# A two-layer graph transformer on one core: gather distance and raw chunks of layer 2, and the order of work at the ends of the span

## The chip, the cores and the metric

One core of a Trainium2 chip runs the whole program. A core has five engines that work side by side, each through its own instruction stream in order: TensorE (PE in the profile; PEld are its weight loads), VectorE (DVE), ScalarE (ACT), GpSimd (POOL) and SyncE (SP). DMAs are issued from SP, ACT and POOL, and 16 DMA engines carry them out. The metric is the device time of one execution in microseconds (us), as a median of runs.

## What is computed

The reference takes 6250 nodes with 128 features, and 106,250 edges sorted by their destination `dst`, each with 64 attributes and a weight. An edge's attributes are joined with 32 cosines of a time difference; two attention layers with two heads follow, with a normalisation over all nodes and a relu between them; at the end the input is added and each node's row is normalised.

```python
def _transformer_conv(h, edge_attr, src, dst, Wq, bq, Wk, bk, Wv, bv, We, Ws, bs):
    q, k, v = ((h @ W + b).reshape(n, H, C) for W, b in ((Wq, bq), (Wk, bk), (Wv, bv)))
    e = (edge_attr @ We).reshape(-1, H, C)
    alpha = einsum('ehc,ehc->eh', q[dst], k[src] + e) / sqrt(C)
    ex = exp(alpha - segment_max(alpha, dst)[dst])
    a = ex / segment_sum(ex, dst)[dst]
    return segment_sum((v[src] + e) * a[:, :, None], dst).reshape(n, H * C) + h @ Ws + bs

rel_t = last_update[src] - t
edge_attr = concatenate([cos(rel_t[:, None] * time_w + time_b), msg], axis=-1)
h = _transformer_conv(x, edge_attr, src, dst, ...)
h = relu((h - h.mean(0)) / sqrt(((h - h.mean(0)) ** 2).mean(0) + 1e-05) * bn_g + bn_b)
out = layernorm(x + _transformer_conv(h, edge_attr, src, dst, ...))
```

## The kernel before

The planning stage in `tile_gnn_resnorm` cuts the sorted edges into 106 chunks (`NC`) of at most 1024 edges (8 rows of 128, `T`) and 64 destination nodes. It tests that the input fits this plan; here it does, and `ordered` runs (`general` is the way for other inputs and isn't run).

**The planning stage** also makes what layer 1 starts from. `load_features` (L505) loads x in four pieces of 12 blocks each into the tile `fhT` from SP's queue, with the times of the nodes behind the first piece, and last the rows left over (`fxrest`, L515 to L517). `pass_features` (L520) writes x with the times in front to the DRAM table `xv_d`: the left-over rows first (L528), then the four pieces, each copied by VectorE or ACT in turn (L530) and stored from SP (L531). It is a generator, and the lines from L1306 on decide where its steps fall between the first table (`tables`, L622, also a generator, with five steps), the edge indices (`columns`, L1312) and the rest.

**Layers 1 and 2** are two calls of `conv` (c = 0 and 1), each a loop of rounds (L964) in which the order of every engine is written by hand. In round k:

- `fetch` (L720) loads the edge attributes of a chunk to come into its buffer `ff`, and its table `ftab`; in layer 2 also the encoded times, the turned edge attributes of layer 1 (`et_d`) and the residual rows (L738 to L744).
- `gather` (L746) fetches the source nodes' rows with eight indirect DMAs from POOL, one for 128 edges. `bring` (L971) places them over the round and ties most to a step of TensorE (`behind`), so that they keep its pace. `lead` (L758) says how many chunks ahead: 4 in layer 1, 2 in layer 2. The buffer `ff` exists five times in layer 2.
- `score(k, 0)`, `turn_weights(k - 1)` and `score(k, 1)` are matmuls for the chunk's scores and the transposes of the weights of the chunk before; `lowest` and `weigh` (VectorE, ACT) make the exponentials; `turn_in(k + 1, ·)` transposes the gathered rows of the next chunk; `divide`, `finish_turn` and `finish` close chunk k - 2; `gather_sums(k - 1)` (L867) sums chunk k - 1 by sixteen matmul instructions.
- `pull(extra, n)` (L1019) takes n steps of other work: in layer 1 the tables of later nodes and, near the end, `pass_rows` or `put_rows`, which transpose finished columns of `fhT` and store them as rows of `h_d`; in layer 2 `block` (L1145): a table block in four steps, then the residual rows, then steps with nothing, seven in all.

Layer 2's nodes are read from two tables. `h_d` holds the raw results of layer 1. `hn_d` holds them after normalisation and relu. It is made in 13 row blocks by `hide` (L769: four transposes on TensorE, a copy on VectorE into one of four `fhn` buffers, a store from SP), three blocks in the round before round 0 and five each in rounds 0 and 1 (L1017). The first `RAW` = 4 chunks are gathered from `h_d` instead, and get the normalisation afterwards, in `turn_in` for the scores and by three VectorE operations in `normalise` (L883) for the sums.

**The end.** `finish` of layer 2 subtracts each row's mean; the squares' sum is closed for a group of chunks at once by a Sqrt on ACT (L939 to L941). `STARTS` lists the first chunk of each group: ten chunks a group up to 96, then 97 to 101, 102 to 104, and 105. `store` (L945) scales a closed chunk on ACT and stores it from SP, one to four a round (L1028). Neighbouring chunks overlap in `out`, so each store waits for the one before.

Of the kernel before, what the change touches and what calls it, by code (L numbers as in the profile page):

```python
# [13 lines left out]
P = 128  # L14
# [30 lines left out]
T = 8  # L45
CE = T * P
NN = P // H
NC = 106
# [7 lines left out]
HIGHEST = 2.0 ** 119  # L56

LG = 10
STARTS = (*range(0, 91, LG), 97, 102, 105)


@with_exitstack
# [439 lines left out]
def load_features(nc, pl, mw, x, node_vec):  # L502

    N = x.shape[0]
    NF = N // P  # L505
    NR = N - NF * P
    xall = pl.xall = pl.hT[:, :NF * D].rearrange("p (b d) -> p b d", d=D)
    pl.cuts = list(zip(range(0, NF, 12), [*range(12, NF, 12), NF]))
    for b0, b1 in pl.cuts:
        nc.sync.dma_start(xall[:, b0:b1], x[:NF * P, :].rearrange("(p b) d -> p b d", b=NF)[:, b0:b1])  # L510
        if b0 == 0:
            pl.times = mw.tile([P, NF], F32, name="fnv", bufs=1)
            nc.sync.dma_start(pl.times, node_vec[:NF * P].rearrange("(p b) -> p b", b=NF))
    if NR:
        nc.vector.memset(pl.rest, 0.0)  # L515
        nc.sync.dma_start(pl.rest[:NR, 1:], x[NF * P:N, :])
        nc.sync.dma_start(pl.rest[:NR, 0:1], node_vec[NF * P:N].rearrange("(p a) -> p a", a=1))  # L517


def pass_features(nc, pl, mw, dram, N):  # L520

    NF = pl.xall.shape[1]
    pl.xv_d = dram.tile([N, 1 + D], F32, name="xv_d")
    rows = mw.tile([P, NF, 1 + D], F32, name="fxrows", bufs=1)
    nc.vector.tensor_copy(rows[:, :, 0], pl.times)
    to = pl.xv_d[:NF * P, :].rearrange("(p b) d -> p b d", b=NF)
    if N > NF * P:
        nc.sync.dma_start(pl.xv_d[NF * P:N, :], pl.rest[:N - NF * P])  # L528
    for i, (b0, b1) in enumerate(pl.cuts):
        (nc.scalar.copy if i % 2 else nc.vector.tensor_copy)(rows[:, b0:b1, 1:], pl.xall[:, b0:b1])  # L530
        nc.sync.dma_start(to[:, b0:b1], rows[:, b0:b1])  # L531
        yield

# [127 lines left out]
def ordered(ctx: ExitStack, tc: tile.TileContext, pl, x, dst, edge_attr_64, conv2, bn_g, bn_b, out):  # L661
# [30 lines left out]

    SINGLE = 40

    RAW = 4

    hidden = list(range(-(-N // GE)))

    def conv(c, extra, first_blocks=None):
# [56 lines left out]
        shape = [P, T, TD]  # L756

        def lead(k):  # L758
            return 2 if c else AHEAD

        def yield_first(bring):
            if not c:
                bring(range(T))
                return
            bring(range(5))
            bring(range(5, T), pl.step)
            first_blocks()
# [66 lines left out]
        def score(k, u):  # L834

            s = ch[k]
            if u == 0:
                s.ps = p_s.tile([P, CE], F32, name="fps")
            w = slice(u * GE, (u + 1) * GE)
            half = nc.tensor.matmul(s.ps[:, w], s.tab[:, :, 0], s.ft[:, w], start=True, stop=False)  # L840
            return half, nc.tensor.matmul(s.ps[:, w], s.tab[:EC, :, 1], s.et[:, w], start=False, stop=True)  # L841
# [120 lines left out]
        with cs, tc.manual_schedule():  # L962
            ended = None
            for k in range(-lead(-NC), NC + 3):  # L964
                def on(j):
                    return 0 <= j < NC

                coming = [j for j in range(k + lead(k - 1), k + lead(k) + 1) if on(j)]
                filling = False

                def bring(rows, behind=None):  # L971
                    for j in coming:
                        gather(j, rows, behind)

                for j in coming:
                    fetch(j)
                if k == -lead(-NC):
                    yield_first(bring)
                elif k < -1:
                    bring(range(T))  # L980
                elif not filling:
                    bring(range(1), ended)
                step = score(k, 0)[1] if on(k) else hide(1) if c and k == -1 else None
                if k >= -1 and not filling:
                    bring((1,), step)
                step = turn_weights(k - 1) if on(k - 1) else hide(1) if c and k == -1 else None
                if k >= -1 and not filling:
                    bring((2,), step)
                place()
                if on(k - 2):  # L990
                    divide(k - 2)
                half, step = score(k, 1) if on(k) else (hide(1) if c and k == -1 else None, None)
                if k >= -1 and not filling:
                    bring((3,), half if c else step or half)
                    if c:
                        bring((4,), step)
                if on(k - 2):
                    finish_turn(k - 2)
                if on(k):
                    lowest(k)  # L1000
                step = turn_in(k + 1, 0) if on(k + 1) else None
                if k >= -1 and not c:
                    bring(range(5) if filling else (4,), step)
                if on(k):
                    weigh(k)
                step = turn_in(k + 1, 1) if on(k + 1) else None
                if k >= -1:
                    bring((5,), step)
                for j in (k + 2,) if k < SINGLE else (k + 2, k + 3) if k == SINGLE else (k + 3,):
                    if c == 0 and on(j):  # L1010
                        encode(j)
                        if j < SINGLE + 3:
                            sine()
                if k >= 0:
                    at_round[0] = k
                    if c and k < 2:
                        hide(5)  # L1017
                    else:
                        pull(extra, 2 if k < 4 or k > 96 else 1)  # L1019
                if len(args) == 3 or args and k == NC - 4:  # L1020
                    sine()
                if on(k - 2):
                    finish(k - 2)
                if c and on(k):
                    if k < RAW:
                        normalise(k)
                    nc.vector.tensor_copy(ch[k].f[:, :, 1 + D:1 + D + TD], ch[k].z)
                for _ in range(min(len(done), 4 if k >= NC else 2 if k > NC - 12 else 1)):  # L1028
                    store(*done.pop(0))
                *steps, ended = gather_sums(k - 1) if on(k - 1) else (None, None, None)  # L1030
                if k >= -1:
                    for t, step in zip((6, 7), steps):
                        bring((t,), step)
            at_round[0] = 2 * NC
            for _ in extra:
                pass
            for rows in done:
                store(*rows)
# [146 lines left out]
def tile_gnn_resnorm(ctx: ExitStack, tc: tile.TileContext, x, src, dst, edge_attr_64, edge_weight, node_vec,  # L1185
# [13 lines left out]
    with tc.tile_pool(name="plan", bufs=1) as pl, tc.tile_pool(name="planw", bufs=2) as mw, \  # L1199
# [140 lines left out]
        next(first_table)  # L1340
        next(first_table)
        next(passed)
        for _ in first_table:
            pass
        columns(flats[0], srcs)
        for _ in passed:
            pass
        got.tw = broadcast(nc, keep, "ftw", time_w, TD)
        got.tb = broadcast(nc, keep, "ftb", time_b, TD)
        nc.sync.dma_start(got.wv[0], conv1["Wv"])  # L1350
# [55 lines left out]
```

## Time and profile before

Three runs: median 2306.39 us, from 2305.79 to 2308.45. The execution that was profiled took 2306.31 us.

| what | us |
|---|---|
| the profiled execution, device time | 2306.31 |
| its span, first to last instruction | 2304.3 |
| granted TensorE clock, mean over the span | 0.983 |
| planning, layer 1's first gather on POOL | 39.25 |
| layer 1's last gather from xv_d | 1132.2 |
| layer 2's first gather from h_d | 1184.96 |
| layer 2's first gather from hn_d | 1232.29 |
| layer 2's last gather | 2266.08 |
| last store issued | 2298.65 |

| stretch, us | TensorE busy | VectorE busy | ACT busy | POOL busy | granted clock | DMA share |
|---|---|---|---|---|---|---|
| 0 to 60 | 34.61 | 30.89 | 19.25 | 20.87 | 0.77 | 0.74 |
| 300 to 700 | 397.62 | 281.33 | 272.33 | 295.91 | 1.00 | 0.64 |
| 1100 to 1180 | 74.53 | 43.46 | 39.55 | 25.20 | 1.00 | 0.39 |
| 1180 to 1240 | 45.12 | 29.50 | 26.40 | 36.60 | 0.86 | 0.82 |
| 1240 to 1300 | 56.29 | 25.08 | 20.09 | 42.66 | 0.97 | 0.71 |
| 1700 to 2000 | 296.10 | 117.81 | 133.25 | 226.90 | 1.00 | 0.68 |
| 2240 to 2270 | 25.74 | 7.78 | 10.56 | 18.68 | 0.89 | 0.59 |
| 2270 to 2304 | 20.26 | 10.68 | 12.06 | 0.00 | 0.87 | 0.04 |

A line of a group in the profile reads: line of the code, engine, operation, tile written and tile read, count, then busy time, mean length of one in ns, and the idle time of that engine just before, with what ended most of it. A line of a timeline reads: start, length, engine, line, operation, tiles, count, and in brackets the idle time before it. Busy time isn't the whole cost of an instruction: the step from one to the next on the engine counts too.

### The profile page before, as it was taken

The numbers are of one execution on the slowest core, as the hardware profiler recorded it, in microseconds if no ns is written. First come the engines' busy times: TensorE is split into PE (matmuls) and PEld (weight loads), VectorE is DVE, ScalarE is ACT, GpSimd is POOL, SyncE is SP. The second block draws the span as 40 slices with busy tenths as digits, with TensorE's granted clock in tenths as the row PEclk, the third lists the DMA queues.
The fourth block names the chain that finished last, engine by engine and source line by source line (L and its number), as shares of the span: only waits on it lengthen the run. The fifth ranks groups of instructions, "written<-read, shape, count | busy, mean of one in ns | idle before, by whom it ended". The sixth has DMA issues, their size and how long they took to land.

```text
span 2304.3 us, 40495 instructions
## 1 busy us (share of the span) xinstructions
PE 2210.9 (96%) x11589; PEld 1707.9 (74%) x11589; DVE 1243.7 (54%) x3745; ACT 1227.9 (53%) x1951; POOL 1628.7 (71%) x1717
## 2 busy tenths in 40 slices
PE   5999999999999999999978999999999999999996
PEld 3687888778887888888856777777777776777775
DVE  5576767676676767777635333433334343343332
ACT  3677777776666665555643444444444444444443
POOL 3777777777777777777536777777777777777772
PEclk7899999999999999999989999999999999999998
DMA  7666666656666666666548656676676676666562
GB/s 231 167 179 171 173 190 178 187 143 180 187 176 179 160 191 172 179 179 168 146 121 219 172 153 181 184 183 174 170 190 184 173 188 165 178 180 162 152 168 51
DMA packets 431095, 396.64 MB, mean 172 GB/s; under 512 B 279682, under 2 KB 375167, under 8 KB 427535
## 3 DMA queue, kind: packets, MB, share of 16 engines
q1 hardware_dynamic: 357648, 239.69, 38.1%
q0 software_dynamic: 54656, 113.07, 20.5%
q10 hardware_dynamic: 18558, 41.20, 5.0%
q8 instruction: 95, 1.56, 0.3%
q14 instruction: 138, 1.12, 0.2%
HBM read 277.16 MB, written 113.14 MB: 169 GB/s over the span
## 4 chain that ended last, share of the span: by engine, by line
PE 67%; DMA 6%; POOL 2%; issue 2%; DVE 1%; SPq 0%; ACT 0%; POOLq 0%; DVEq 0%; ACTq 0%
PE fpa L871 22%; PE fps L840 11%; PE fps L841 11%; PE fpx L819 6%; PE fppt L863 6%; DMA ff<-hn_d,fsrcs 5%; PE fpg L627 3%; PE fpe L828 2%; POOL ff L749 2%; PE fpo L921 2%; PE fpo L922 1%; PE fpo L893 1%; PE fpo L894 1%; PE fpo L903 1%; PE fpo L904 1%
## 5 line engine op out<-in xcount | busy, mean ns | idle before, releaser
L749 POOL DMA_INDIRECT ff<-xv_d,fsrcs x848 | 817.7, 964 | 304.0 <-issue 100.0
L749 POOL DMA_INDIRECT ff<-hn_d,fsrcs x816 | 775.6, 950 | 265.4 <-issue 107.1
L871 PE MATMUL fpa<-ff,fpt 128*128 128x225 f32 x3392 | 693.3, 357 | 0.0
L871 PEld LDWEIGHTS fpa<-ff,fpt 128*128 128x128 f32 x3392 | 627.4, 190 | 11.2 <-issue 0.7
L864 ACT COPY fpt<-fppt 128x512 f32<-128x512 f32 x424 | 228.0, 590 | 472.2 <-PE fppt L863 467.4
L840 PE MATMUL fps<-fft,ftab 128*128 128x512 f32 x848 | 442.9, 604 | 0.6 <-ACT fs L853 0.6
L823 ACT COPY fft<-fpx 128x512 f32<-128x512 f32 x416 | 242.1, 582 | 365.3 <-PE fpx L819 365.2
L896 DVE COPY fat<-fpo 128x256 f32<-128x256 f32 x212 | 90.1, 425 | 586.0 <-PE fpo L894 556.3
L853 ACT ACTIVATE fs<-fps,fm 128x1024 f32<-128x1024 f32 x212 | 236.3, 1114 | 85.8 <-DVE fm L848 83.4
L819 PE MATMUL fpx<-fident,ff 128*128 128x128 f32 x1696 | 248.2, 276 | 34.6 <-DMA ff<-hn_d,fsrcs 26.3
L863 PEld LDWEIGHTS fppt<-fident,fs 128*128 128x128 f32 x1696 | 198.4, 141 | 104.7 <-issue 103.6
L846 DVE TENSOR_REDUCE flow<-fps 128x1 f32<-128x1024 f32 x212 | 257.5, 1214 | 10.0 <-PE fps L841 10.0
L819 PEld LDWEIGHTS fpx<-fident,ff 128*128 128x128 f32 x1696 | 197.9, 141 | 46.4 <-DMA ff<-hn_d,fsrcs 34.3
L841 PE MATMUL fps<-fxT,ftab 112*128 112x512 f32 x424 | 218.4, 596 | 2.1 <-DMA fxT<-et_d 2.1
L863 PE MATMUL fppt<-fident,fs 128*128 128x128 f32 x1696 | 220.0, 272 | 0.0
L841 PE MATMUL fps<-fet,ftab 112*128 112x512 f32 x424 | 217.9, 595 | 0.0
L840 PEld LDWEIGHTS fps<-fft,ftab 128*128 128x128 f32 x848 | 166.6, 226 | 3.8 <-issue 2.2
L841 PEld LDWEIGHTS fps<-fet,ftab 112*128 112x128 f32 x424 | 106.5, 251 | 76.0 <-issue 58.7
L841 PEld LDWEIGHTS fps<-fxT,ftab 112*128 112x128 f32 x424 | 83.9, 198 | 102.0 <-issue 94.9
L794 DVE SCALAR_TENSOR_TENSOR farg<-fturns,farg 128x256 f32<-128x256 f32 x318 | 135.4, 426 | 10.9
L878 DVE TENSOR_SCALAR finv<-fpa 128x1 f32<-128x1 f32 x212 | 33.5, 158 | 191.7 <-PE fpa L871 185.3
L828 PE MATMUL fpe<-fident,ff 128*112 128x128 f32 x848 | 129.1, 275 | 1.5 <-DVE ff L806 1.5
(216 smaller groups left out, 2348.6 us busy)
## 6 DMA issues: line engine op xcount, KB each, us to landing
ff<-in_edge_attr SPq DMA_DIRECT2D x212, 256.0 KB
et_d<-fet SPq DMA_DIRECT2D x106, 448.0 KB
fxT<-et_d SPq DMA_DIRECT2D x106, 448.0 KB
ftab<-tab_d SPq DMA_DIRECT2D x106, 192.0 KB
tab_d<-fo ACTq DMA_DIRECT2D x13, 1536.0 KB
ff<-xv_d,fsrcs POOLq DMA_INDIRECT x848
enc_d<-fzs SPq DMA_DIRECT2D x106, 128.0 KB
ftab<-tab_d SPq DMA_DIRECT2D x106, 128.0 KB
```

The costliest lines, as they stand in the source:

```text
L749: row = nc.gpsimd.indirect_dma_start(out=f[:, t, (1 if c else 0):1 + D], out_offset=None, in_=(h_d[:N, :] if k < RAW else hn_d) if c else ...
L794: nc.vector.scalar_tensor_tensor(arg, turn, -part, arg, op0=OP.mult, op1=OP.add)
L819: last = nc.tensor.transpose(px[:, t * P:(t + 1) * P], s.f[:, u * 4 + t, 1:1 + D], ident)
L823: nc.scalar.copy(s.ft[:, u * GE:(u + 1) * GE], px)
L828: last = nc.tensor.transpose(pe[:EC, t * P:(t + 1) * P], s.f[:, u * 4 + t, 1 + D:], ident)
L840: half = nc.tensor.matmul(s.ps[:, w], s.tab[:, :, 0], s.ft[:, w], start=True, stop=False)
L841: return half, nc.tensor.matmul(s.ps[:, w], s.tab[:EC, :, 1], s.et[:, w], start=False, stop=True)
L846: nc.vector.tensor_reduce(low, s.ps, AX.X, OP.min)
L853: nc.scalar.activation(s.s, s.ps, AF.Exp, bias=s.bias, scale=-1.0)
L863: last = nc.tensor.transpose(pp[:, t * P:(t + 1) * P], s.s[:, at:at + P], ident)
L864: nc.scalar.copy(s.pt[:, u * GE:(u + 1) * GE], pp)
L871: nc.tensor.matmul(s.pa, s.pt[:, t * P:(t + 1) * P], s.f[:, t, 1:1 + D + EW], start=t == 0, stop=t == T - 1)
```

## The change

- **Distance and raw chunks.** `lead` is 3 in layer 2, and `RAW` is 6, so the first six chunks are gathered from `h_d`. The fill before round 0 takes three steps: chunk 0 as before; chunk 1, its eight gathers in pairs between three row blocks; chunk 2 behind the transposes of chunk 0 (`filling`).
- **Row blocks.** Three before round 0, then four, three and three in rounds 0, 1 and 2. The table steps that stood in rounds 2 and on begin in round 3: three there, two each in rounds 4 and 5, then one as before.
- **End of layer 1.** In its round `NC + 1` the two steps of `extra` (the row blocks 11 and 12 of `h_d`) also stand ahead of `finish_turn` and `finish` of the last chunk.
- **Start.** The left-over rows and their times are loaded ahead of x. The fourth piece of `xv_d` is copied by VectorE and not by ACT, after the first table's third step and ahead of its last steps and of the edge sources.
- **End.** The last groups are 97 to 100, 101 and 102, and 103, 104 and 105 alone.

```diff
 LG = 10
-STARTS = (*range(0, 91, LG), 97, 102, 105)
+STARTS = (*range(0, 91, LG), 97, 101, 103, 104, 105)
...
     pl.cuts = list(zip(range(0, NF, 12), [*range(12, NF, 12), NF]))
+    if NR:
+        nc.vector.memset(pl.rest, 0.0)
+        nc.sync.dma_start(pl.rest[:NR, 1:], x[NF * P:N, :])
+        nc.sync.dma_start(pl.rest[:NR, 0:1], node_vec[NF * P:N].rearrange("(p a) -> p a", a=1))
     for b0, b1 in pl.cuts:
...
-    if NR:
-        nc.vector.memset(pl.rest, 0.0)
-        nc.sync.dma_start(pl.rest[:NR, 1:], x[NF * P:N, :])
-        nc.sync.dma_start(pl.rest[:NR, 0:1], node_vec[NF * P:N].rearrange("(p a) -> p a", a=1))
...
-        (nc.scalar.copy if i % 2 else nc.vector.tensor_copy)(rows[:, b0:b1, 1:], pl.xall[:, b0:b1])
+        (nc.scalar.copy if i == 1 else nc.vector.tensor_copy)(rows[:, b0:b1, 1:], pl.xall[:, b0:b1])
...
-    RAW = 4
+    RAW = 6
...
         def lead(k):
-            return 2 if c else AHEAD
+            return 3 if c else AHEAD
...
-                filling = False
+                filling = c and k == -1
...
                     yield_first(bring)
+                elif k < -1 and c:
+                    for t in range(0, T, 2):
+                        bring((t, t + 1), hide(1) if t else None)
                 elif k < -1:
...
-                step = score(k, 0)[1] if on(k) else hide(1) if c and k == -1 else None
+                step = score(k, 0)[1] if on(k) else None
...
-                step = turn_weights(k - 1) if on(k - 1) else hide(1) if c and k == -1 else None
+                step = turn_weights(k - 1) if on(k - 1) else None
...
-                half, step = score(k, 1) if on(k) else (hide(1) if c and k == -1 else None, None)
+                if c == 0 and k == NC + 1:
+                    at_round[0] = k
+                    pull(extra, 2)
+                half, step = score(k, 1) if on(k) else (None, None)
...
-                if k >= -1 and not c:
+                if k >= -1 and not c or filling:
                     bring(range(5) if filling else (4,), step)
...
-                    if c and k < 2:
-                        hide(5)
+                    if c and hidden:
+                        hide(4 if k == 0 else 3)
                     else:
-                        pull(extra, 2 if k < 4 or k > 96 else 1)
+                        pull(extra, (3 if k == 3 else 2) if c and k < 6 else 2 if k < 4 or k > 96 else 1)
...
         next(passed)
+        next(first_table)
+        for _ in passed:
+            pass
         for _ in first_table:
             pass
         columns(flats[0], srcs)
-        for _ in passed:
-            pass
```

## Prediction

> **What bounds the kernel now.** I read the engine shares and slices first, then the groups by line, the stretches by engine, the gather engine's own timeline, the chain of waits, and last the queues at both ends of the span.
>
> ```profile
> PE 2210.9 (96%) x11589; PEld 1707.9 (74%) x11589; DVE 1243.7 (54%) x3745; ACT 1227.9 (53%) x1951; POOL 1628.7 (71%) x1717
> L749 POOL DMA_INDIRECT ff<-hn_d,fsrcs x816 | 775.6, 950 | 265.4 <-issue 107.1
> L819 PE MATMUL fpx<-fident,ff 128*128 128x128 f32 x1696 | 248.2, 276 | 34.6 <-DMA ff<-hn_d,fsrcs 26.3
> ```
>
> TensorE at 96% looks like the bound. In layer 1 it is: from 300 to 1050 us it idles 2.4 us. In layer 2 the second line decides. A row gather keeps POOL 0.95 us and 0.30 us lies before the next one even when nothing is waited for, so 1.25 us a gather, 10.0 us for a chunk's eight; POOL's 71% counts only the 0.95. A round of TensorE lasts 9.28 us without a piece of tables (sums at 1262.45, 1271.73, 1281.01 in the chain of waits) and 10.14 us with one (1311.99 to 1322.13). Of the seven pulls per table block five carry TensorE work, so a round means (5 x 10.14 + 2 x 9.28)/7 = 9.89 us, under POOL's 10.0. So layer 2 is bound by gather issue, and TensorE's waits (third line) are its shadow. What can be won there is POOL's real idle time:
>
> ```profile
> 1223.82 0.95 POOL L749 DMA_INDIRECT ff<-h_d,fsrcs  x1 [0.30 <-PE fpa L871]
> 1225.07 0.95 POOL L749 DMA_INDIRECT ff<-h_d,fsrcs  x1 [0.30 <-issue]
> 1232.29 0.95 POOL L749 DMA_INDIRECT ff<-hn_d,fsrcs  x1 [6.27 <-DMA hn_d<-fhn]
> 1233.54 0.95 POOL L749 DMA_INDIRECT ff<-hn_d,fsrcs  x1 [0.30 <-PE fpx L819]
> ...
> 2251.37 0.94 POOL L749 DMA_INDIRECT ff<-hn_d,fsrcs  x1 [0.67 <-PE fpx L819]
> 2254.22 0.95 POOL L749 DMA_INDIRECT ff<-hn_d,fsrcs  x1 [1.90 <-PE fpa L871]
> 2255.69 0.95 POOL L749 DMA_INDIRECT ff<-hn_d,fsrcs  x1 [0.53 <-PE fpa L871]
> ```
>
> The bracket is idle time and what ended it; 0.30 is the normal gap. Over the 848 gathers from 1184.96 to 2266.08 the excess above 0.30 sums to 17.9 us: 1.2 at 1192.41 (chunk 0), 6.0 for the normalised rows (above), 3.2 at 1253.51, 1.1 at 1336.60, 0.7 at 1470.06, 1.2 at 1605.43, 2.6 from 2251 to 2259, and 1.9 in eleven small ones. Both ends:
>
> ```profile
> SPq L528 <- DMA fxrest<-in_node_vec: 14.1, 1, 14.1
> 38.72 1.02 ACT L653 COPY fxT<-fpx 128x512 f32<-128x512 f32 x1 [10.13 <-DMA xv_d<-fxrows]
> ...
> 2290.19 2.36 SPq L956 DMA_DIRECT2D out<-fout  x2
> 2295.59 0.47 SPq L956 DMA_DIRECT2D out<-fout  x1
> 2298.65 0.48 SPq L956 DMA_DIRECT2D out<-flast  x1
> ```
>
> At the start SP stands 14.1 us for a tiny load that lies last in its queue, then the copies wait for the xv_d writes behind it. At the end the last store leaves at 2298.65, though its rows were ready at 2295.31: it waits for the store before it.
>
> **The change, part by part.** Everything is taken off the profiled execution: 2306.31 us, its span 2304.3 plus 2.0 around it, which equals the median 2306.39 within 0.1.
>
> *Three chunks ahead, six raw chunks, rows in three rounds.* Gathers and their pacing steps keep their number; chunk k+3 is issued where k+2 was. In the fill the order of POOL is the old one (chunks 0, 1, 2, 3 back to back from 1184.96 to 1225.07), so the 1.2 us of chunk 0 stay. Chunks 4 and 5 now read raw rows: the 6.0 us go. Chunk 6 is the first to need hn_d; POOL reaches it at 1226.3 + 2 x 10.0 = 1246.3. The last hn_d store now stands on SP behind the fetch of chunk 5 in round 2, whose buffer frees at the end of the sums of chunk 0 (about 1225); register reads, five issues and four stores (4.4 us a fetch in the rows at 1232 to 1237, 0.4 to 0.9 a store) bring it to about 1231, landed by about 1235, since the last one in the trace was issued at 1228.2 and released POOL at 1232.29. So 11 us of cover.
>
> The other 10.7 us are gathers that waited for TensorE. They can wait no more if POOL runs late against its pace. Starts of TensorE's rounds, worked forward from 1199.0 (round 0): the rounds 0 to 2 hold four, three and three row blocks (about 0.76 us each), round 3 three table pieces, round 4 two; I get 1213, 1225, 1236, 1248, 1259, 1268. POOL starts the chunk of rounds 1 to 6 at 1226, 1236, 1246, 1256, 1266, 1276: 7 to 13 us late each time, and gains another 7 x 10.0 - 69.3 = 0.7 us of lateness per table block. TensorE first waits when that lateness passes about 11 us (a row is allowed 8.2 us into round k-2 and needed 5 us into round k: 18.6 + 5 - 8.2 less some 4 of landing); before it was about 2. So POOL never stops, and TensorE waits for it once the slack is used. TensorE alone would be done sooner (101 rounds x 9.28 + 12 x 4.37 of tables = 990 us from 1236, against POOL's 1013), so it isn't the bound. Layer 2: -(6.0 + 10.7) = -16.7 us. Bounds: -10 if half of the small waits come back, -20 if the few gathers of 1.1 to 1.5 us also fall.
>
> The last row of chunk 105 then starts at 2266.08 - 16.7 = 2249.4. Before, its transposes ended 5.0 us after it (2271.1), not waiting for it. Now they do: a row landed 2.5 us after its start at 2233.51, at worst 7.07 (2243.51, two fetches at once). I take 3.5, nearer to the first since fetches are now held a round apart by their buffer, plus 0.5 to transpose: -1.0 (from -2.0 to +2.6). The Trainium skill, "DMA: Bandwidth & Descriptors", Anatomy of one DMA, gives 2.0 us plus bytes over 436e3, which is an estimated 2.15 us for 64 KB; with it the total would be 1.4 us lower.
>
> Hidden edits, at nothing: three VectorE operations more for chunks 4 and 5 (2 x 1.22 + 0.69 = 3.1 us each), under VectorE's 35 idle us between 1240 and 1300; without that cover 3.1 us a round. Row blocks, table pieces: only moved. The fetch now waits on SP for the sums of k-2, behind it the tab, z, et and residual loads and the round's output store: needed three rounds later, 20 us of cover. VectorE's memset waits for the same sums as the division behind it does anyway.
>
> *Start.* Loads keep DMA full to 22 us, then it falls to 0.39 and 0.26 until SP's wait ends at 24.28, and the writes run from 26 to 38. With the small loads first, the first three writes can start by 22 and the fourth is copied by VectorE near 24.8 and not by ACT at 27.12 to 28.59. The writes and the table (3.1 + 1.6 MB at some 420 GB/s, as from 26 to 36 us) then end near 33. The two small loads now push the x loads back by their issue, 0.27 + 0.44 us; the first copy, at 9.71, follows VectorE's own work and covers it. But VectorE's planning ends at 33.95 and takes the 0.95 us copy on top, so the xT copies start about 35.1 instead of 38.72: -3.6 (from -5 to +1, the copy's cost if nothing lands earlier). Layer 1 is bound by TensorE fed from these, so it passes through.
>
> *End of layer 1.* Two row blocks leave 1.0 us earlier on SP, ahead of the last hT store (1179.79) and of the h_d rows (1181.43), on which the first gather waits. VectorE's two copies (0.89) push the last result by 0.3: -0.8. Bound: TensorE now stands at these transposes until the hT store of 1173.09 landed, at the latest 1176.81 where they ran unhindered: +0.95; the other end -1.2.
>
> *Tail.* Chunk 104 closes alone, so its store leaves near 2289.8 and not 2295.59, and the last one goes when ready. Price: the close of chunk 103 puts a table load (1.28) and Sqrt between VectorE's statistics and the division of chunk 104: reciprocal at 2284.45, division at 2284.75 and not 2284.14, +0.7 on the closing chain. Last store 2295.31 + 0.7 + 0.4 = 2296.4 against 2298.65: -2.2 (from -3 to +1). A rule speaks against it: the Trainium skill, "ScalarE: Activation LUTs", What ACT_TABLE_LOAD costs, asks to group by table set and prices a switch at 2.66 us with its drain. The trace shows 1.283 us and Exp 0.02 us after its load (2272.73 to 2272.75), no drain; two switches more would by the rule be up to 5.3 us and the tail +3.
>
> Sum: -16.7 - 1.0 - 3.6 - 0.8 - 2.2 = -24.3; 2306.3 - 24.3 = **2282 us**.
>
> **Rivals.** *The waits come back* (the change does less than it says): gathers still stop at TensorE's pace because the five buffers are exactly full; only the 6.0 and the 3.2 go, the ends give 6.6: 2306.3 - 15.8 = 2290. For it: a gather of k+3 needs the buffer of k-2, free only as the round begins. Against: POOL is 7 us late there. *TensorE becomes the bound*: were the 0.30 gap a wait that lead removes, layer 2 ends 22 us earlier still, 2260. Against: 0.30 is the least gap in layer 1 too. *Nothing gained*: if what POOL wins is lost to slower landings, 2305. *SP sets the round*, the slower side: its fetch can no longer run ahead of the sums; if a fetch (4.4) and store (2 at most) took over 10.24 us a round, 102 rounds x 0.24 eat the 24 us; at 10.5 it is 2306.3 - 24.3 + 51 = 2333. The rows add to 6.4 us, so far from it.
>
> **Chances.** Forecast 0.78, own range 2276 to 2290; waits come back 0.13; TensorE bound 0.03; nothing 0.02; SP 0.04. A measurement here tells 0.2% (4.6 us) from no change. Faster 0.94, same 0.02, slower 0.04. Range 2274 to 2295: the forecast with its unknown landings and ends, and the first rival.
>
> **What would show it.** Right: 48 gathers from h_d and 800 from hn_d; no wait for hn_d before the first of these; POOL's gaps at 0.30 from chunk 1 to chunk 105; its last gather about 21 us earlier (layer 2 and both earlier ends); TensorE still waiting on gathered rows; xT copies near 35; the last two stores over 6 us apart. Wrong: gaps on POOL ended by TensorE in rounds 3 to 100, TensorE waiting for fxT, ftab or fr, a wait for hn_d at chunk 6, or a last store held by ACT's tables.

## The result and the profile after

The changed kernel takes 2288.26 us, median of six runs (2284.05 to 2289.69); the kernel before took 2306.56 (2303.14 to 2310.41) in the six runs beside it. The ratio is 0.9916, 95% interval 0.9905 to 0.9928: 18 us faster, 6 less than the 24.3 of the forecast. The six runs stand at two places, two near 2284.2 and four from 2288.1 to 2289.7; the profiled one is of the lower (2284.39, its span 2282.6).

The page of the changed kernel, engine shares and two groups by line:

```profile
PE 2204.2 (97%) x11589; PEld 1705.5 (75%) x11589; DVE 1244.6 (55%) x3756; ACT 1230.0 (54%) x1954; POOL 1625.4 (71%) x1717
...
L749 POOL DMA_INDIRECT ff<-hn_d,fsrcs x800 | 758.7, 948 | 243.8 <-issue 85.9
...
L819 PE MATMUL fpx<-fident,ff 128*128 128x128 f32 x1696 | 245.3, 275 | 26.1 <-DMA ff<-hn_d,fsrcs 15.7
```

The idle time before an hn_d gather was 265.4 us over 816 gathers and is 243.8 over 800, which is 0.305 each: the bare gap. TensorE still waits for gathered rows, 15.7 us instead of 26.3; its share of the span stays as high as it was, so it tells nothing of the gain. POOL's timeline where the normalised rows are first read (start, length, engine, line, operation, tiles, count, idle time before):

```profile
1243.65 0.95 POOL L749 DMA_INDIRECT ff<-h_d,fsrcs  x1 [0.30 <-issue]
1244.90 1.31 POOL L749 DMA_INDIRECT ff<-h_d,fsrcs  x1 [0.30 <-issue]
1246.51 0.98 POOL L749 DMA_INDIRECT ff<-hn_d,fsrcs  x1 [0.30 <-DMA ff<-h_d,fsrcs]
```

Chunk 6 goes on without a stop where chunk 4 stood 6.27 us before, and it starts at 1246.51, where the working had 1246.3. Over all of layer 2 the time above 0.30 is 1.6 us, in one gather of chunk 0, against 17.9.

Both ends, first SP's and then ScalarE's timeline:

```profile
2.95 0.24 SPq L511 DMA_DIRECT2D fxrest<-in_x  x1
...
6.23 0.37 SPq L514 DMA_DIRECT2D fhT<-in_x  x1
```

```profile
37.65 1.02 ACT L653 COPY fxT<-fpx 128x512 f32<-128x512 f32 x1 [9.15 <-DMA tab_d<-fo]
```

```profile
2261.18 1.28 ACT L853 ACT_TABLE_LOAD   x1 [3.13 <-DVE fm L848]
...
2263.90 1.28 ACT L940 ACT_TABLE_LOAD   x1
```

The first piece of x left at 2.99 us before and leaves at 6.23 now, because SP stands 2.6 us between the small loads and it (before, it stood as long behind that piece, 3.35 to 5.93). The xT copy, at 38.72 before, now ends its wait on a write of tab_d and not of xv_d. At the tail both table loads stand between the last scores and the last close. The one for the last Exp comes 3.13 us after ScalarE's work before it, when VectorE's result for that Exp is there. Two chunks earlier the load ran ahead of that result:

```profile
2241.84 1.28 ACT L853 ACT_TABLE_LOAD   x1
...
2242.39 0.15 DVE L848 TENSOR_SCALAR fm<-flow 128x1 f32<-128x1 f32 x1
```

Of the 87 loads for Exp in this profile 84 start 0.2 to 0.7 us before `fm` is written. For the last Exp of each layer alone the wait for `fm` is an instruction of its own (two EVENT_SEMAPHORE of L853, at 1165.7 and 2261.1 us), and the second of them stands ahead of the load.

### The profile page after: what moved, and what is told of

It is laid out like the page before. It is cut to its first block, busy times and chain, and to the rows that moved or that the text cites. A ratio compares the mean times of both kernels' runs of the same rounds, so it can differ in the third digit from the quotient of the medians.

```text
span 2282.6 us, 40553 instructions
## 1 busy us (share of the span) xinstructions
PE 2204.2 (97%) x11589; PEld 1705.5 (75%) x11589; DVE 1244.6 (55%) x3756; ACT 1230.0 (54%) x1954; POOL 1625.4 (71%) x1717
## 3 DMA queue, kind: packets, MB, share of 16 engines
q1 hardware_dynamic: 357648, 239.69, 38.6%
## 4 chain that ended last, share of the span: by engine, by line
PE 45%; DMA 4%; issue 1%; DVE 1%; POOL 0%; ACT 0%; SPq 0%; POOLq 0%; DVEq 0%; ACTq 0%
PE fpa L871 16%; PE fps L840 8%; PE fps L841 8%; PE fpx L819 4%; PE fppt L863 4%; DMA ff<-hn_d,fsrcs 3%; PE fpg L627 2%; PE fpo L921 2%; PE fpo L922 1%; PE fpo L893 1%; DMA ff<-h_d,fsrcs 1%; PE fpo L894 0%; PE fpg L1146 0%; POOL ff L749 0%; DMA fhT<-fres 0%
## 5 line engine op out<-in xcount | busy, mean ns | idle before, releaser
L749 POOL DMA_INDIRECT ff<-hn_d,fsrcs x800 | 758.7, 948 | 243.8 <-issue 85.9
L853 ACT ACTIVATE fs<-fps,fm 128x1024 f32<-128x1024 f32 x212 | 236.3, 1115 | 81.0 <-DVE fm L848 79.2
L819 PE MATMUL fpx<-fident,ff 128*128 128x128 f32 x1696 | 245.3, 275 | 26.1 <-DMA ff<-hn_d,fsrcs 15.7
```

Source lines behind the costliest of these rows:

```text
L749: row = nc.gpsimd.indirect_dma_start(out=f[:, t, (1 if c else 0):1 + D], out_offset=None, in_=(h_d[:N, :] if k < RAW else hn_d) if c else ...
L819: last = nc.tensor.transpose(px[:, t * P:(t + 1) * P], s.f[:, u * 4 + t, 1:1 + D], ident)
L853: nc.scalar.activation(s.s, s.ps, AF.Exp, bias=s.bias, scale=-1.0)
```

## The experiments

Six profiles come from chips on which the kernel before takes 2305 to 2307 us. The table cuts their spans at the same five events, read off the timelines of POOL, TensorE and SP: the first gather of layer 1, its last one, the first gather of layer 2, the end of the transposes of chunk 105's last row, the issue of the last store. The last column is POOL's idle time above 0.30 us in layer 2. The profile of raw6_only is of its slowest run (2311.29 us).

| kernel | to 1st gather | layer 1, 1st to last gather | to layer 2's 1st gather | to chunk 105's last row turned | to last store's issue | span | POOL's excess |
|---|---|---|---|---|---|---|---|
| before | 39.2 | 1092.9 | 52.8 | 1086.3 | 27.4 | 2304.3 | 17.9 |
| raw6_only | 38.5 | 1096.8 | 53.3 | 1087.6 | 27.8 | 2309.5 | 18.5 |
| ends_only | 38.3 | 1095.7 | 52.5 | 1085.3 | 26.0 | 2304.3 | 21.8 |
| l2_only | 38.9 | 1095.1 | 53.2 | 1070.4 | 27.7 | 2290.9 | 0.5 |
| after | 38.2 | 1091.9 | 52.3 | 1068.5 | 26.0 | 2282.6 | 1.6 |
| after_again | 39.5 | 1095.3 | 52.3 | 1067.4 | 26.0 | 2286.2 | 1.1 |

**l2_only: layer 2's edits without the ends**

```diff
 # the kernel before, with
-    RAW = 4
+    RAW = 6
-            return 2 if c else AHEAD
+            return 3 if c else AHEAD
 # and the row blocks and table steps of the change
```

> The kernel before with the parts in layer 2 alone: three chunks ahead, six chunks from raw rows, row blocks over three rounds. The start, the order of layer 1's last rounds and the list of Exp chunks stay as before. My theory (the layer-2 chain of gathers gave nearly all): first gather of layer 2 at 1185 us as before, chain of gathers 1065 us as in the changed kernel (1081 before), so 16 to 18 us off, 2289 to 2291. Rival (the ends carry more than their parts, because layer 2 starts later and its first rounds then wait again): a chain of over 1070 us and no more than 12 us off, 2294 or more.

Measured 2291.38 us (six runs, 2286.32 to 2293.96) beside 2305.42 of the kernel before (23 runs): 0.9938, 0.9925 to 0.9951, which is 14.3 us off with 11.3 to 17.3 as its interval. In the profile layer 2 is 15 to 17 us shorter than in the three kernels with the old layer 2, its chain of gathers is 1063.7 us, and POOL's excess is 0.5. The theory holds in the stages: layer 2 doesn't wait again when it starts later. The time lies 0.4 us above the theory's range; in the profile layer 2 starts at 1187.3 us and not at 1185, since layer 1 was 2.2 longer than in the profile before.

**ends_only: the ends without layer 2's edits**

```diff
 # the kernel before, with
-STARTS = (*range(0, 91, LG), 97, 102, 105)
+STARTS = (*range(0, 91, LG), 97, 101, 103, 104, 105)
 # the start's order, and in round NC + 1 of layer 1
+                if c == 0 and k == NC + 1:
+                    at_round[0] = k
+                    pull(extra, 2)
```

> The kernel before with the three ends alone: the rest rows' loads first and the copies' engines at the start, layer 2's first gathers after one round less at the end of layer 1, two more Exp chunks at the tail. My theory, from the two traces: 1.6 us at the start, 0.95 at the end of layer 1; the tail's 1.5 only if POOL's last gathers are early enough for it, so 2.5 to 4.1 us off, 2302.5 to 2304. Rival (the ends gave what the prediction said, 3.6 + 0.8 + 2.2): 6.6 off, 2300. Second rival: what is gained before layer 2 is lost in layer 2's first rounds, because the chunk that waits for its normalised rows waits for TensorE's layer-1 rows anyway: 1 us off or less.

Measured 2305.58 (11 runs): 0.9998, 0.9988 to 1.0008, from 2.8 us off to 1.8 more. The second rival fits the time: the ends alone give nothing that these runs can tell. The stages say why it can't be 6.6. The tail is 1.4 to 1.8 shorter and layer 1's end 0.2 to 0.7, but the start's 38.3 is only 0.2 to 0.9 under the 39.2, 38.5 and 38.9 of the old order, and after_again, with the new one, has 39.5. The rival's reason isn't in the profile: layer 2, 1085.3, is no longer than with the old ends, and the 2.8 us that layer 1 took more hide the small gains.

**raw6_only: six raw chunks, still two ahead**

```diff
-    RAW = 4
+    RAW = 6
```

> The kernel before with one number changed: the first six chunks of layer 2 take raw rows instead of four, still two chunks ahead. My theory (two separate losses before: 6.0 us of waiting for normalised rows, 10.7 us of POOL going at TensorE's pace because it is only two chunks ahead): the 6.0 goes or turns into waits for a free buffer, 3 to 6 us off, 2300.5 to 2303.5, and gathers still show idle time ended by TensorE. Rival (the raw rows alone give it all): 14 us off or more, 2292. Second rival (nothing without the third chunk of lead: POOL is stopped by the buffers at once): under 1.5 us off.

Measured 2305.17 (11 runs): 0.9998, 0.9989 to 1.0007. The second rival holds, and my split of the loss into two was wrong. POOL's timeline at chunk 4 of this kernel:

```profile
1234.94 0.94 POOL L749 DMA_INDIRECT ff<-h_d,fsrcs  x1 [0.30 <-issue]
1237.77 0.94 POOL L749 DMA_INDIRECT ff<-h_d,fsrcs  x1 [1.89 <-PE fpx L819]
1242.12 1.73 POOL L749 DMA_INDIRECT ff<-h_d,fsrcs  x1 [3.41 <-PE fpa L871]
```

The 6.0 us for the normalised rows are gone, and two waits for TensorE's steps, 1.6 and 3.1 above the gap, stand in the same chunk; the sum over layer 2 is 18.5 where it was 17.9. With two chunks of lead POOL was at TensorE's heels and had to stop somewhere; the wait for hn_d was only the first place.

**after_again: the changed kernel once more**

> The changed kernel as it is, to see its spread beside the others: its six runs stood at two places, 2284.1 to 2284.4 twice and 2288.1 to 2289.7 four times. If the two belong to the kernel, both come again, with 4 us between them; if they belong to the chip of that day, this run stands at one. The profile of a run near 2288 would say where the 4 us lie: in the start's transfers, in POOL's gathers (each 5 ns longer over 800 would do), or in TensorE's rounds.

Measured 2289.40 (five runs, 2287.89 to 2290.23): 0.9933, 0.992 to 0.9945. All five stand at the higher place, and the profile is one of them. Against the first profile its span is 3.6 longer: 1.3 at the start, 3.4 in layer 1, 1.1 less in layer 2. At its gather 800 layer 1 is 0.7 us behind, and the other 2.7 are lost behind that, at one place. TensorE's timeline there, and TensorE and its clock from 1110 to 1120 us (stretch, length, then busy time and count for TensorE, its weight loads, VectorE, ScalarE and POOL, then granted clock, DMA share, GB/s), for the changed kernel's first profile:

```profile
1106.33 0.33 PE L1068 MATMUL fpg<-fident,fhT 128*128 128x128 f32 x1 [1.65 <-DMA fhT<-fres]
```

```profile
1110.00:1120.00 10.00, 10.00 (x56) 8.33 (x56) 6.41 (x18) 5.51 (x8) 7.56 (x9) 1.00 0.61 174
```

and for after_again:

```profile
1109.40 0.47 PE L1068 MATMUL fpg<-fident,fhT 128*128 128x128 f32 x1 [2.42 <-DMA fhT<-fres]
```

```profile
1110.00:1120.00 10.00, 10.00 (x45) 8.11 (x45) 4.35 (x16) 1.91 (x5) 5.68 (x7) 0.86 0.60 165
```

TensorE turns a block of rows of which the last chunk has only just been stored, and waits for the landing. After 1.65 us it goes on at full clock, with 56 matmuls from 1110 to 1120; after 2.42 the clock is 0.86 there, with 45. Where it is low it is so in one piece: from 1109.39 to 1112.80, 3.41 us, the profile has 0.50. The six profiles line up: waits of 1.65 and 1.75 (before) with a clock of 1.00 and a layer 1 of 1091.9 and 1092.9; waits of 2.12 (ends_only), 2.42, 2.52 (l2_only) and 4.77 (raw6_only) with 0.83 to 0.91 and 1095.1 to 1096.8. The kernel before has this wait too, so it is no part of the change. That the wait causes the low clock is the likely reading; the run made to remove it, calm, couldn't show it.

**On other chips.** The remaining eight kernels ran on three other chips. There the kernel before takes 2685 to 2690 us, and all of it is slower, layer 1 too: 1274 to 1290 us from its first to its last gather. What was expected for 2305 can't be read from those times, only from stretches.

**calm and calm_pairs: that row block one round later; with the tail's shorter list**

```diff
-                while at_round[0] < 3 + k:
+                while at_round[0] < 3 + k + (k > 90 and b0 not in ends):
 # calm_pairs, besides
-STARTS = (*range(0, 91, LG), 97, 101, 103, 104, 105)
+STARTS = (*range(0, 91, LG), 97, 102, 104, 105)
```

> The changed kernel with one row block of layer 1 (the last that is written before the layer's end) turned one round later. In five of the six profiles so far TensorE stands 1.7 to 2.5 us, once 4.8 us, at about 1105 us for the landing of the rows of the chunk just finished, and where it stands 2.4 us or more the granted clock is down to 0.84 to 0.86 in the ten us behind; the last gather of layer 1 comes 1091.8 and 1092.9 us after the first in the two profiles with 1.7 and 1.8 us, 1095.2 to 1096.8 in the others. My theory (this one wait and what the clock loses after it make most of the spread between runs, and of the 4 us between the changed kernel's two places): the wait is gone, 1090 to 1092 us, and the median 2.5 to 4 us below the changed kernel's 2288 to 2289, 2284.5 to 2286.5. Rival (the clock's loss only moves to another wait): 2288 or more, with a low clock elsewhere in layer 1. Second rival: the block comes too late for the last rounds, and layer 2 starts 2 us or more later.

> The changed kernel with two edits: the last row block written inside layer 1 turned one round later, and the tail's list ..., 97, 102, 104, 105; the start as in the changed kernel. On a chip on which the kernel before takes 2300 to 2310. My theory: TensorE's wait of 1.7 to 2.4 us for the finished rows at 1105 us is gone, layer 1 takes 1090 to 1092 us from the first to the last gather in every run, and the tail's stretch 24.6 to 25.0 us; together 3 to 5 us under the changed kernel (2288 to 2289), 20 to 22 us under the kernel before, and a spread of the runs of 3 us or less. Rival (the clock is lost at another place all the same, as it already is at some runs after the 2.4 us wait at 503 us): 1094 or more, 2287 or more. On a chip like the second and third, on which the kernel before takes 2685, neither can be told.

calm 2688.92 beside 2689.49 (0.9996, 0.9978 to 1.0014), calm_pairs 2687.70 beside 2689.07 (0.9992, 0.9974 to 1.0009). Neither says anything on the 4 us: layer 1 has some 200 us of other stops there. Whether the edit removes them stays open.

**tail_pairs: the shorter list alone**

> The changed kernel with the tail's list of chunks after which the output's square root is taken one shorter, ..., 97, 102, 104, 105 for 97, 101, 103, 104, 105. From the last row transposed of chunk 105 to the issue of the last store took 26.0 and 26.1 us in the two profiles of the changed kernel, 27.6 in the one of the kernel before. My theory (both table loads, 1.28 us each, stand on that stretch since Exp comes back after chunk 104's square root; with chunk 103 and 104 under one square root one goes): 24.6 to 25.0 us, 1.2 us off, which the times can hardly tell. Rival (chunk 103's rows then wait and come out later, on the store queue of SP): 26 us or more.

2687.71 beside 2689.49 (0.9996, 0.9975 to 1.0016). The time can't tell, the stretch can. The last row's transposes in TensorE's timeline, for this kernel and, with the longer list on the same chip, for calm:

```profile
2655.95 1.03 PE L819 MATMUL fpx<-fident,ff 128*128 128x128 f32 x8
```

```profile
2648.10 1.03 PE L819 MATMUL fpx<-fident,ff 128*128 128x128 f32 x8
```

From their end to the issue of the last store it is 24.8 us here (2656.98 to 2681.75) and 26.0 in calm (2649.13 to 2675.15), as in the changed kernel: the theory's range. calm_pairs and best, with the shorter list, have 24.8 too; untied and lead_raw4, with the longer one, have 27.4 and 27.7. ScalarE's timeline shows why:

```profile
2667.27 1.11 ACT L853 ACTIVATE fs<-fps,fm 128x1024 f32<-128x1024 f32 x1 [3.15 <-DVE fm L848]
...
2668.69 1.28 ACT L940 ACT_TABLE_LOAD   x1
```

The last Exp starts as its input comes, with no load between. From there to the last store's issue at 2681.75 it is 14.5 us; in calm it is 15.75 from the load's start (2659.40 to 2675.15).

**best: calm_pairs, and the first piece of x ahead of the small loads**

```diff
 # besides calm_pairs: the loads of pl.rest stand behind
 # the first piece of x and fnv, ahead of the other three
```

> The changed kernel with three edits, each read at its own stretch of the trace: the last row block written inside layer 1 turned one round later; the tail's list ..., 97, 102, 104, 105; and at the start the two loads of the rest rows behind the first piece of x instead of ahead of it (still ahead of the other three). On a chip on which the kernel before takes 2300 to 2310: (1) layer 1, first to last gather, 1090 to 1092 us without the wait for the finished rows, against 1091.8 and 1095.3 of the changed kernel; rival: 1094 or more. (2) last row transposed of chunk 105 to the issue of the last store 24.6 to 25.0 against 26.0 and 26.1; rival: 26. (3) first piece of x issued at 3.0 to 3.5 us instead of 6.2, first layer-1 gather at 36 to 37.5 instead of 38.2 to 39.5; rival (the start hangs on the tables' path, tab_d, not on x): 38 or later. Sum by my theory: 4 to 6 us under the changed kernel, 2283 to 2285 and 21 to 24 us under the kernel before; by the rivals 2288. On a chip where all engines stall for long, as on the second one, nothing can be told from the time.

2686.27 beside 2685.08 (0.9996, 0.9974 to 1.0019; the medians lie the other way): no difference that can be told. The start can be read on the slower chips too, since calm's first gather, at 38.6, lies as early as in the table. SP's and ScalarE's timelines:

```profile
2.96 0.36 SPq L510 DMA_DIRECT2D fhT<-in_x  x1
```

```profile
38.30 1.02 ACT L653 COPY fxT<-fpx 128x512 f32<-128x512 f32 x1 [8.53 <-DMA tab_d<-fo]
```

x's first piece leaves 3.3 us earlier than in the changed kernel and the copy is no earlier, still behind tab_d; the first gather comes at 38.8. The rival holds. The other three pieces of x left later here (9.53 us instead of 7.60), so this doesn't clear x's delay altogether.

**lead_raw4: three ahead, four raw chunks**

```diff
-    RAW = 6
+    RAW = 4
+                if filling:
+                    hide(5)
-                        hide(4 if k == 0 else 3)
+                        hide(5)
```

> The changed kernel with four chunks from raw rows as before instead of six, the lead of three kept; the row blocks are spread 3, 5, 5 over the rounds ahead of chunk 1, so that all are written before chunk 4 is gathered. On a chip on which the kernel before takes 2300 to 2310: my theory (the lead does the work; the raw rows only cover the time until the normalised rows are written): POOL waits once, at chunk 4, 3 to 8 us, since it comes there a round earlier than with a lead of two, and then goes on at 1.25 us a gather without another wait, chain of gathers 1067 to 1072 us (1063.7 to 1065.4 with six, 1081 to 1082 before), 3 to 7 us slower than the changed kernel, 2291 to 2295. Rival (both parts are needed, as neither of the kernels with one of them gains): the wait at chunk 4 uses up the third chunk of lead and POOL goes at TensorE's pace from there, 1078 us or more, 2300 or more. Second rival (raw rows are worth nothing): within 2 us of the changed kernel.

2698.36 beside 2685.08: 1.0037, 1.0019 to 1.0055, where best, in the same set, is at 0.9996. POOL stands once at chunk 4:

```profile
1427.33 1.16 POOL L749 DMA_INDIRECT ff<-hn_d,fsrcs  x1 [11.09 <-DMA hn_d<-fhn]
```

That is 10.8 us above the gap, more than the 3 to 8 expected, and the time pays for all of it (12 us over best). So the longer lead needs the raw chunks; that they need it in turn raw6_only has shown. How much of the gain is left with a lead of three and four raw chunks where the kernel before takes 2305 wasn't measured. And no run has the new lead and the six raw chunks with the old spread of row blocks and table steps, so what moving these is worth by itself isn't shown.

**after_seven, before_seven: an eighth of layer 2's gathers left out**

```diff
 # in gather(), ahead of the indirect DMA, in each of the two kernels
+                if c and t == T - 1:
+                    nc.sync.dma_start(f[:, t, 1:1 + D], (h_d if k < RAW else hn_d)[:P, :])
+                    continue
```

> The changed kernel, in which the last of the eight rows of each layer-2 chunk is no gather on POOL but a plain load on SP's queue of the first 128 rows of the table: an eighth of layer 2's gathers are left out (and the values with them). My theory (after the change POOL's 10.0 us a chunk sets layer 2, against 9.89 of TensorE, so there is only 0.1 us a chunk to win): POOL's part falls to 8.75, TensorE takes over at 9.89, 106 x 0.11 = 12 us off, and the waits for the last rows (some 4 us) with it: 12 to 16 us off the changed kernel, 2272 to 2277. Rival (TensorE or the landing of rows sets the round already): 3 us off or less, 2285 or more. Second rival (POOL's pace is all of it): 130 us off, which TensorE's 9.89 excludes unless its rounds are stretched by waiting for rows.

> The same row taken off POOL in the kernel before, two chunks ahead. My theory (the lead of two is too short only because POOL is as slow as TensorE; with 8.75 us a chunk POOL waits and loses nothing): within 6 us of the same edit on the changed kernel after the ends' 4 us are counted, 2276 to 2286, so 20 to 30 us off the kernel before. Rival (two chunks of lead stall TensorE by themselves, whatever POOL's pace): 10 to 15 us slower than the same edit on the changed kernel, 2284 or more, the gathers' landing still waited for by TensorE.

2556.60 and 2561.25 beside 2689.49 (0.9503, 0.9481 to 0.9525; 0.9516, 0.9495 to 0.9538): 133 and 128 us off, which the first of the two had only as an excluded rival. From its first to its last gather layer 2 takes 1133.7 and 1143.0 us there against 1270.6 with eight (calm and tail_pairs), 10.7 and 10.8 a chunk against 12.0. So a chunk is POOL's gathers at 1.25 us plus 2 us, with seven as with eight, and each gather left out is saved whole. On TensorE's pace where the kernel before takes 2305, the question they were made for, they say nothing.

**untied: gathers held by a free buffer alone**

```diff
-                if behind is not None:
+                if behind is not None and not (c and k >= RAW):
```

> The changed kernel in which the gathers of layer 2 from chunk 6 on are no longer held behind a step of TensorE in their round; what holds them is a free buffer alone (five for three chunks ahead). Where the kernel before takes 2305: POOL has no wait for TensorE left in layer 2 (1.6 us in all), so within 2 us of the changed kernel's 2288 to 2289. Where it takes 2685 (TensorE, VectorE and ScalarE stand there for 2 to 6 us at a time, and POOL then waits for TensorE's step at rows 5 to 7 of the chunk, 172 to 184 us of its 209 in layer 2): my theory (POOL needs 10.0 us of every round, so each such wait adds to its chain and is never made up; with 8.75 us a chunk the chain went from 1270.6 to 1133.7) is that the waits at rows 1 to 7 shrink to under 40 us, POOL's chain comes to 1130 to 1190 us, and the time to 2550 to 2610, 75 to 135 under the kernel before. Rival (the buffers hold POOL as well): the waits move to row 0 of the chunks, 2670 or more. Second rival (each gather itself disturbs the other engines there, 1.25 us apiece, whenever it comes): chain 1250 or more, 2665 or more, with POOL's waits under 100.

2682.51 beside 2689.81: 0.998, 0.9965 to 0.9995. The chain is 1264.8, and of POOL's 202.0 us of waits 192.4 stand at row 0: the first rival. A chunk's last gather and the first of the next, from the timeline of this kernel:

```profile
1709.02 0.95 POOL L749 DMA_INDIRECT ff<-hn_d,fsrcs  x1 [0.30 <-issue]
...
1709.47 1.02 PE L841 MATMUL fps<-fxT,ftab 112*128 112x512 f32 x2
...
1712.27 0.14 DVE L878 TENSOR_SCALAR finv<-fpa 128x1 f32<-128x1 f32 x1 [5.07 <-issue]
...
1712.40 1.07 ACT L864 COPY fpt<-fppt 128x512 f32<-128x512 f32 x2 [4.68 <-remote]
...
1712.49 0.95 POOL L749 DMA_INDIRECT ff<-hn_d,fsrcs  x1 [2.53 <-remote]
...
1713.25 0.39 PE L893 MATMUL fpo<-fident,fa 128*128 128x128 f32 x1 [2.76 <-DVE fa L881]
```

VectorE's finv needs only the sums that TensorE ended near 1706, ScalarE's copy the transposes ended at 1708.8, and POOL's gather a free buffer; all three start within 0.22 us of each other, 2.3 us after POOL's last gather ended (1709.97). "issue" and "remote" say that the profile has nothing that released them. Twelve us on (1724.36, 1724.49, 1724.58) the same three start together again. This is the 2 us of a chunk. What holds the engines isn't shown. Nor does the stop belong to the end of a chunk's gathers: in layer 2 of this kernel 86 of the 89 stretches of over 1 us in which VectorE, ScalarE and POOL all stand begin behind a chunk's last gather, but in calm, whose gathers are tied to TensorE's steps, 65 of 81 begin behind the fifth, sixth or seventh and none behind the last. The place moved with the order of the gathers; POOL's waits stayed, 202.0 us here and 208.6 there.

## Why the prediction came out as it did

**What set layer 2: right, in mechanism and size.** The forecast had 16.7 for the chain of gathers and 1.0 for the last row's landing, 17.7 in all. The same stretch in the table is 17.8 shorter in the first profile of the changed kernel and 18.9 in the second. The signs named are there: 48 and 800 gathers, no wait for hn_d at chunk 6, bare gaps from chunk 1 on, TensorE still waiting for rows; the last gather came 18.3 us earlier (2247.77) where about 21 was said. Two inner divisions were off without moving the sum. The chain gave 15.7 in the first profile (1081.1 to 1065.4) and the landing 2.0. From the last gather's start to its transposes' end the kernel before took 5.2 us (to 2271.26, not 2271.1); ends_only, with the old lead, also has 3.1, and l2_only, with the new one, 6.7, so that part isn't the lead's, and that two errors of 1 us cancelled is luck. And the 6.0 and 10.7 us weren't two losses: one loss, POOL at TensorE's heels, showed itself at several places.

**The rival "the waits come back" had the better time and the wrong reason.** It said 2290, and the medians are 2288.26 and 2289.40. But POOL's excess is 1.1 to 1.6 us, not the 8.7 it would leave (17.9 less 6.0 and 3.2). A time near a rival's number is no evidence for it; its mark in the trace is.

**The start: mis-sized, and the larger error.** The step said that with the small loads first the xT copies start near 35.1, 3.6 us earlier. They start at 37.65. The writes of xv_d did cease to be the gate, as said, but two other chains lie close behind. One is the write of tab_d, which the step had inside the same sum; it is the gate in this profile. The other is VectorE's planning: TensorE's transposes for these copies wait for it, and start at 35.0 to 36.2 us in the three profiles with the new order, at 33.2 to 33.8 with the old. The copy named needs eight of them, done 1.9 us later at 36.95, so even without tab_d it could not have started near 35.1; in ends_only and after_again the profile names these transposes as the gate. x's first piece went from 2.99 to 6.23 us, where the step had 0.7 us of issue, and the DMA share fell to 0.54 between 6 and 8 us; best, with that piece early again, starts its copies no earlier. Over three profiles with the old order and three with the new the first gather comes at 38.9 and 38.7 us: worth 0.2, not 3.6.

**The end of layer 1** measured 0.4 in the pair and 0.7 as a mean of three against three; 0.8 was said. **The tail** measured 1.4 for 2.2. The step counted one table load on the closing chain. There are two, since for the last Exp the wait for VectorE stands ahead of the load; the division of chunk 104 came 1.9 us after its sums (2263.78 to 2265.70) where the step's times have 0.6. tail_pairs takes one load out and has its 1.2 us back.

**The rest is run to run.** The sum of these terms gives the profile: 2.5 less at the start, 0.8 at the tail and 0.4 at the end of layer 1, 0.1 more in layer 2 and 1.1 more in layer 1, so 21.7 us of span instead of 24.3. The median lies 3.9 above that profile; the second profile, a run of the higher place, has 3.4 more in layer 1 and 1.3 more at the start. The base of the forecast, the profiled run of the kernel before, had itself the short wait (1.75). Nine of the changed kernel's eleven runs stand at the higher place, and a forecast from one profile can't see which place the median will take.

**Where it doesn't hold.** On the three slower chips the changed kernel as it is wasn't timed; with small edits of its ends or of layer 1's end (calm, tail_pairs, calm_pairs, best) it stands at 0.9992 to 0.9996 of the kernel before, no gain within 0.3%. The forecast rests on POOL finding TensorE's steps done. Where a chunk has some 2 us in which VectorE, ScalarE and POOL stand, the third chunk of lead gave POOL nothing; why they stand is open.

## What to carry over

When two engines need nearly the same time for a round (10.0 and 9.89 us here), waits between them are one loss that moves: removing the largest (raw6_only) brought nothing, and the longer lead without cover for its first need (lead_raw4) cost 12 us, on a chip where the whole change gains nothing; both together, with the row blocks moved, took 15 to 17 us off layer 2. Before an early transfer is moved, list every chain that meets at the gate; one that lies within a few us behind takes the gain. Cut several profiles of a kernel at the same events before a few us are read from one of them, and look at a second chip before a gain is called a property of the kernel.

## What the runs showed of the hardware

- The granted clock was 0.83 to 0.91 from 1110 to 1120 us after a wait of TensorE of 2.12, 2.42, 2.52 or 4.77 us, and 1.00 with one of 1.65 or 1.75; each fall is one piece of 0.50 for 3.41 us. At 503 us a wait of 2.37 stands in all six profiles, with a clock of 0.91 from 500 to 520 us in three of them and 1.00 in the other three.
- The Trainium skill, "TensorE: Matmul & The Clock Gate", Part 1, lets the clock fall after at least one idle window of about 3.4 us; here it fell behind 2.1 to 2.5 us, and the measurement decides.
- A table load of 1.28 us can run while its activation's input isn't there yet: 84 of 87 loads for Exp start 0.2 to 0.7 us before that input is written. Where the wait was an instruction ahead of the load, it came whole on top: 3.13 us idle, then the load, then Exp.
- One program took 2305 us on one chip and 2685 to 2690 on three others, with equal lengths of the single gather (median 0.945 and 0.947 us) and about 2 us more for a chunk, as a mean, in both layers.
